# Seven 128x128 products in place of four 128x256 in a projection, reciprocals spread by DMA, one score tile lowered by VectorE

## The chip, the cores and the metric

The kernel runs on one core of a Trainium2 chip. The metric is the device time of one execution in microseconds (us); lower is better. The kernel before the change takes 997.76 us, the median of three runs.

In what follows PE is TensorE, DVE is VectorE, ACT is ScalarE, POOL is GpSimd and SP is SyncE, which here only issues DMAs. PSUM is the memory that PE writes; DVE and ACT can read it, POOL cannot. SBUF is the working memory of all of them.

## The reference

A cross-attention block in fp32, for 16 batches of 1024 query rows and 64 context rows, width 512, 16 heads of 32:

```
xq  = (1 + scale_q) * layernorm(x)       + shift_q     # scale, shift from silu(cond) @ Wss
xkv = (1 + scale_kv) * layernorm(ctx)    + shift_kv
q = xq @ Wq + bq ;  k, v = split(xkv @ Wkv + bkv)
p = softmax(q k^T / sqrt(32))                          # per head, over 64 keys
out = x + ((p v) as rows of 512) @ Wp + bp
```

## The kernel before, in words

**Blocks.** The query rows are cut into 32 blocks of 512 rows, two to a batch. A block passes through these steps: normalise (`hidden`, ACT), transpose (`turn` on DVE and `move`, 16 DMAs), scale (`scale_features`, ACT), query projection (`query_product`, `quarter_products`, PE), scores (`score_products`, PE), maxima (`maximum` and `maxima`, DVE), subtraction of the maxima (`subtract`, POOL), exponentials (`weights` and `again`, ACT), the sum over the keys (`total` on POOL, `row_total` on DVE), the product with the values (`mix`, PE), the division by the sum (`divided`, DVE) and the output projection (`product`, PE, with `added` on DVE).

**Fewer products.** Each 512x512 projection is cut into halves and made by a scheme with seven half-size products instead of eight. Products are numbered 1 to 7. Their operands include sums and differences of halves, which POOL makes (`row_sum` for the rows `ot`, `feature_sums` for the features), and their results are added up in PSUM in a fixed order. In the output projection products 1, 6, 5 and 3 go into PSUM bank 2 one after the other, products 2, 7 and 4 into bank 3. After each product `added(i, n)` (DVE, L1116) adds the bank's present content to the output rows `r`, and the next product into that bank waits until `added` has read it. Query products 1 and 7 are already made a second time by this scheme, of seven 128x128 products each: `quarter_products`, with operands from `feature_quarters` (POOL), a copy by ACT (`quarter_copies`) and three adds by DVE in PSUM (`quarter_adds`), before the last three of the seven run. The weight sums for query product 7 are made once, ahead of the loop, by POOL (`weight_quarter_sums(7)`, L565 to L573).

**Loop.** Lines L1587 to L1704 run for i = 3 to 29. An iteration works on several blocks at once: the scores of block i, the output projection of block b = i-2 (products 6, 5, 4, 3) and a = i-1 (products 1, 2, 7), the query projection of block n = i+1, and the preparation of blocks i+2 to i+4. Ahead of the loop the same steps stand written out for blocks 0 to 3, behind it for blocks 30 and 31.

**Order.** The order of the calls in the source is the order of each engine's queue; nothing reorders it. An engine takes its instructions strictly in that order, so an instruction that waits holds all behind it on the same engine. The same holds for the DMAs that SP issues.

**Around the scores.** A block's score tile has two key halves z = 0 and 1, and each lies in two PSUM tiles (e = 0 and 1). There are only two such PSUM tiles in turn; the next `score_products` or `mix` needs them back. They come back when DVE has taken the maxima (L755, 128x1024 at a time) and ACT has copied the scores to SBUF (`copied`, L764). `maxima` then spreads the maxima over 128x2048 (`mb`, L784, a DVE transpose), POOL subtracts `mb` from both halves (L797, 128x2048 each), ACT takes the exponentials, POOL adds the halves (`total`, L858), DVE reduces the sum (`row_total`, L863) and takes its reciprocal (L878).

**Reciprocals.** `inverse_rows` writes the 128x64 reciprocals to DRAM (32 KB) and reads them back in another order (four DMAs of 8 KB into `vr`); `spread_rows`, in the next iteration, spreads them over 128x2048 by a DVE transpose (L891) into `vb`. `divided` (L915, two instructions of 128x1024) multiplies the PSUM result of `mix` by `vb` and leaves `ot` in SBUF.

## Time and profile before

| what | value |
|---|---|
| median of three runs | 997.76 us (997.4 to 999.06) |
| the profiled execution: time / span in the trace | 999.01 us / 996.9 us |
| busy share of the span: PE, DVE, ACT, POOL | 99%, 90%, 78%, 90% |
| first scores of the loop (block 3) on PE | 151.2 us from the span's start |
| one iteration, from block to block | 28.52 us |
| first scores behind the loop (block 30) on PE | 921.4 us |

In rows of the trace the columns are: start in us, duration in us, engine, line, operation, output<-inputs, partitions times elements, count; in brackets the idle time of the engine just before, and what ended it. Rows that stand directly behind one another can be merged ("x2"). In the chain of waits a row is start, duration and what the end of the program hung on at that time. One PE product of the source shows as two records, so "x8" is four products.

### The profile page before, as it was taken

The numbers are of one execution on the slowest core, as the hardware profiler recorded it, in microseconds if no ns is written. First come the engines' busy times: TensorE is split into PE (matmuls) and PEld (weight loads), VectorE is DVE, ScalarE is ACT, GpSimd is POOL, SyncE is SP. The second block draws the span as 40 slices with busy tenths as digits, with TensorE's granted clock in tenths as the row PEclk, the third lists the DMA queues.
The fourth block names the chain that finished last, engine by engine and source line by source line (L and its number), as shares of the span: only waits on it lengthen the run. The fifth ranks groups of instructions, "written<-read, shape, count | busy, mean of one in ns | idle before, by whom it ended". The sixth has DMA issues, their size and how long they took to land.

```text
span 996.9 us, 20564 instructions
## 1 busy us (share of the span) xinstructions
PE 984.2 (99%) x7465; PEld 760.7 (76%) x7465; DVE 895.6 (90%) x1318; ACT 779.3 (78%) x1165; POOL 895.4 (90%) x690
## 2 busy tenths in 40 slices
PE   7999999999999999999999999999999999999998
PEld 6878777787777877877778778777787787777756
DVE  7696899999999999999999999999999999987786
ACT  3878878888888888888888888888888888876620
POOL 2677899999999999999999999999999999999681
PEclk9999999999999999999999999999999999999999
DMA  9765655555655555566655555665555555544422
GB/s 308 264 165 151 156 164 156 140 165 180 190 181 176 159 165 152 151 182 186 183 176 152 173 145 155 185 188 178 176 150 175 151 154 182 148 132 130 145 85 97
DMA packets 115188, 165.77 MB, mean 166 GB/s; under 512 B 34920, under 2 KB 46464, under 8 KB 113168
## 3 DMA queue, kind: packets, MB, share of 16 engines
q1 hardware_dynamic: 114704, 163.93, 55.2%
q8 instruction: 59, 0.97, 0.4%
q0 software_dynamic: 384, 0.54, 0.2%
q14 instruction: 41, 0.34, 0.1%
HBM read 79.47 MB, written 34.60 MB: 114 GB/s over the span
## 4 chain that ended last, share of the span: by engine, by line
PE 88%; DMA 4%; DVE 3%; SPq 2%; POOL 1%; issue 1%; ACT 0%; DVEq 0%; POOLq 0%
PE pp L1086 36%; PE pq L534 27%; PE pq L605 10%; PE ps L738 6%; PE po L936 5%; PE pk_A L534 1%; PE pk_B L534 1%; DMA w_k_sb<-in_L_xcond_Wkv_dram 1%; DMA r<-in_x_dram 1%; PE pv_B L534 1%; DMA ltd<-lt 1%; DMA V_B<-stage_B 1%; DMA vr<-ltd 0%; POOL sum L858 0%; DVE l L826 0%
## 5 line engine op out<-in xcount | busy, mean ns | idle before, releaser
L797 POOL TENSOR_TENSOR s<-s,mb 128x2048 f32<-128x2048 f32 x64 | 290.6, 4564 | 20.3 <-DVE mb L784 13.4
L1086 PE MATMUL pp<-w_p_sb,ot 128*128 128x256 f32 x740 | 174.8, 379 | 1.1 <-DVE ot L915 1.1
L764 ACT COPY s<-ps 128x1024 f32<-128x1024 f32 x128 | 129.3, 1013 | 46.1 <-PE ps L738 34.0
L755 DVE TRANSPOSE_TENSOR_REDUCE m<-ps 128x32 f32<-128x1024 f32 x128 | 152.4, 1228 | 10.4 <-PE ps L738 9.3
L1086 PEld LDWEIGHTS pp<-w_p_sb,ot 128*128 128x128 f32 x740 | 138.2, 190 | 20.5 <-issue 2.8
L645 ACT ACTIVATE qt<-pq,bias_t 128x256 f32<-128x256 f32 x256 | 107.8, 475 | 48.8 <-PE pq L605 27.7
L858 POOL TENSOR_TENSOR sum<-s,p 128x2048 f32<-128x2048 f32 x30 | 136.5, 4549 | 1.6 <-ACT p L808 1.6
L1116 DVE TENSOR_TENSOR r<-pp,r 128x512 f32<-128x512 f32 x183 | 120.3, 669 | 13.8 <-ACT xt L442 6.8
L534 PE MATMUL pq<-xt,w_q_sums 128*128 128x256 f32 x512 | 123.8, 385 | 0.0
L534 PEld LDWEIGHTS pq<-xt,w_q_sums 128*128 128x128 f32 x512 | 95.0, 190 | 34.6 <-issue 22.6
L1086 PE MATMUL pp<-WT,ot 128*128 128x256 f32 x492 | 118.4, 383 | 0.0
L1086 PE MATMUL pp<-WT,s 128*128 128x256 f32 x488 | 116.1, 380 | 1.3 <-DVE r L1107 0.8
L817 ACT ACTIVATE s<-s 32x2048 f32<-32x2048 f32 x60 | 114.6, 1910 | 1.8 <-DMA p<-s 0.4
L1086 PEld LDWEIGHTS pp<-WT,ot 128*128 128x128 f32 x492 | 90.9, 190 | 19.1 <-issue 4.2
L1086 PEld LDWEIGHTS pp<-WT,s 128*128 128x128 f32 x488 | 88.2, 190 | 13.1 <-POOL s L1056 1.3
L327 ACT ACTIVATE x<-x,rstdq 128x512 f32<-128x512 f32 x128 | 94.8, 807 | 1.0 <-POOL rstdq L304 1.0
L442 ACT ACTIVATE xt<-xt,ss_q 128x512 f32<-128x512 f32 x124 | 94.0, 809 | 1.0 <-DMA xt<-ht 0.7
L915 DVE TENSOR_TENSOR ot<-po,vb 128x1024 f32<-128x1024 f32 x62 | 73.0, 1219 | 17.6 <-PE po L936 17.4
L286 DVE BATCH_NORM_STATS2 bs<-x 128x6 f32<-128x512 f32 x128 | 85.3, 666 | 0.0
L493 POOL TENSOR_TENSOR xt_sums<-xt 128x512 f32<-128x512 f32 x64 | 81.2, 1269 | 2.0 <-DMA x<-in_x_dram 1.3
L357 DVE STREAM_TRANSPOSE ht<-x 128x512 f32<-128x512 f32 x124 | 77.7, 679 | 4.7 <-DMA xt<-ht 2.2
L891 DVE STREAM_TRANSPOSE vb<-vr 128x2048 f32<-128x2048 f32 (+1 forms) x33 | 73.7, 2236 | 4.4 <-DMA vr<-ltd 4.4
(224 smaller groups left out, 1963.8 us busy)
## 6 DMA issues: line engine op xcount, KB each, us to landing
x<-in_x_dram SPq DMA_DIRECT2D x32, 1024.0 KB, 5.3
r<-in_x_dram SPq DMA_DIRECT2D x32, 1024.0 KB, 5.9
xt<-ht SPq DMA_DIRECT2D x488, 64.0 KB, 2.0
out_dram<-r SPq DMA_DIRECT2D x60, 512.0 KB, 4.7
p<-s SPq DMA_DIRECT2D x60, 256.0 KB, 3.8
wss_kv<-in_L_xcond_Wss_kv_dram SPq DMA_DIRECT2D x4, 512.0 KB, 7.2
wss_q<-in_L_xcond_Wss_q_dram SPq DMA_DIRECT2D x4, 512.0 KB, 11.0
vr<-ltd SPq DMA_DIRECT2D x128, 8.0 KB, 1.7
```

Source lines behind the costliest of these rows:

```text
L327: nc.scalar.activation(dst, src, AF.Identity, bias=rstd[:, 1, j : j + 1], scale=rstd[:, 0, j : j + 1])
L442: nc.scalar.activation(xt[:, :, c, :], xt[:, :, c, :], AF.Identity, scale=ss["q"][:, c, b : b + 1], bias=ss["q"][:, NC + c, b : b + 1],)
L534: nc.tensor.matmul(out_, lhsT=lhsT, rhs=rhs, start=new and m == 0 and c == 0, stop=c == HC - 1, skip_group_check=True,)
L605: nc.tensor.matmul(qa["q", k][:, q * P : (q + 1) * P], lhsT=lhsT, rhs=rhs, start=first and q == 0, stop=True, skip_group_check=True,)
L645: nc.scalar.activation(dst, src, AF.Identity, bias=bq_t[:, o : o + 1])
L755: nc.vector.tensor_reduce(m_tiles[i][:, z, 2 * e : 2 * e + 2, :], s_banks[i, z][e].rearrange("p r (j a) -> p r j a", a=32), AX.X, ALU.max, ...
L764: nc.scalar.copy(s_tiles[i, z][:, 2 * e : 2 * e + 2, :], s_banks[i, z][e])
L797: eng.tensor_tensor(s_tiles[i, z], s_tiles[i, z], mb_tiles[i], ALU.subtract)
L817: nc.scalar.activation(s_tiles[i, 0][at + 32 : at + 64], raw_tiles[i][at : at + 32], AF.Exp, scale=SCALE)
L858: nc.gpsimd.tensor_tensor(t, s_tiles[i, 0], s_tiles[i, 1], ALU.add)
L1086: nc.tensor.matmul(to, lhsT=rows[:, c, t * P : (t + 1) * P], rhs=cols[:, c, :], start=n == 2 and (i, 2) not in seeded and t == 0 and c == ...
L1116: nc.vector.tensor_add(r, a, r)
```

## The change

1. **Output product 1 of blocks 2 to 28** is made of seven 128x128 products (`row_products`, four first and three later) in place of four 128x256. Its operands are made per block by POOL (`row_quarters`, three instructions); ACT copies two quarters of the bank (`row_copies`), DVE adds three times in PSUM (`row_adds`). The bias that fills bank 2 is reordered for that (`bias_quarters`). Four weight sums for it are made once, ahead of the loop, by DVE (`projection_quarter_sums`), and `weight_quarter_sums(7)` moves from POOL to DVE and stands earlier.
2. **Reciprocals of blocks 2 to 29**: DVE transposes the 128x64 reciprocals, one DMA writes them to DRAM (32 KB), and `spread_rows` reads them back by four DMAs of 256 KB, each value to the 32 partitions and all places where it is needed. The DVE transpose of 128x2048 goes.
3. **One score tile**: for z = 1 and e = 0, DVE subtracts `mb` straight from PSUM (`lowered`, 128x1024); the ACT copy of that tile goes, and POOL's subtraction for z = 1 is halved (`subtract_half`, 128x1024).
4. `row_sum(i, 2)` writes into a part of `ot` that is no longer needed instead of a tile of its own. The order of the calls in the loop is written anew; `added(b, 7)` now opens an iteration. Some calls ahead of the loop change places. Behind the loop all of the first two row groups of `w_p` and the bias are loaded again, and the DVE transpose for block 29 is gone.

```
+    def lowered(i, e):
+        es = slice(2 * e, 2 * e + 2)
+        nc.vector.tensor_tensor(
+            s_tiles[i, 1][:, es, :], s_banks[i, 1][e], mb_tiles[i][:, es, :], ALU.subtract
+        )
...
     def inverse_rows(i):
         lt = lt_tiles.pop(i)
         nc.vector.reciprocal(lt, lt)
...
+        if by_dram(i):
+            t = v.rearrange("p c j -> p (c j)")
+            nc.vector.transpose(t, lt.rearrange("p r j -> p (r j)"))
+            d = rows_dram[i] = dram.tile([2, NC, 2, TB], F32, tag="lb", name=f"lb_{i}")
+            nc.sync.dma_start(
+                d.rearrange("k c e (j a) -> (c e j) k a", a=32),
+                t.rearrange("p (k a) -> p k a", k=2),
+            )
+            return
...
     def spread_rows(i, cs=range(NC)):
+        if by_dram(i):
+            d = rows_dram.pop(i)
+            vb = vb_tiles[i] = qpool.tile([P, NC, TB], F32, tag="vb", name=f"vb_{i}", bufs=1)
+            for r in range(HPC):
+                row = d[r // 2, :, r % 2, :].unsqueeze(0)
+                nc.sync.dma_start(vb[32 * r : 32 * r + 32], row.to_broadcast([32, NC, TB]))
+            return
...
+    def projection_quarter_sums():
+        tt, w = nc.vector.tensor_tensor, p_quarters
+        tt(w[:, 0], weight_block(0, 1), weight_block(0, 0), ALU.subtract)
+        tt(w[:, 2], weight_block(1, 1), weight_block(0, 1), ALU.add)
+        tt(w[:, 1], weight_block(0, 0), w[:, 2], ALU.subtract)
+        tt(weight_block(0, 1), weight_block(1, 0), w[:, 1], ALU.add)
...
+    def row_quarters(i):
+        tt, x, r = nc.gpsimd.tensor_tensor, lambda t, c: row_block(i, t, c), r_quarters
...
+        tt(r[:, 0:2], x(1, 0).unsqueeze(1).to_broadcast([P, 2, P]), others, ALU.subtract)
+        tt(r[:, 2], r[:, 1], x(0, 0), ALU.subtract)
+        tt(ident, x(0, 1), r[:, 2], ALU.add)
...
+    def row_products(i, first):
+        x, r, w = lambda t, c: row_block(i, t, c), r_quarters, p_quarters
+        if first:
+            todo = (
+                (0, x(0, 0), weight_block(0, 0)),
+                (1, r[:, 1], w[:, 0]),
+                (2, r[:, 0], w[:, 2]),
+                (3, r[:, 2], w[:, 1]),
+            )
+        else:
+            todo = (
+                (0, x(0, 1), weight_block(1, 0)),
+                (1, ident, weight_block(1, 1)),
+                (2, x(1, 1), weight_block(0, 1)),
+            )
...
+    def row_adds(i):
+        a, r, tt = acc[2], r_quarters, nc.vector.tensor_tensor
+        both_ = a[:, P : 3 * P].rearrange("p (k n) -> p k n", k=2)
+        tt(r[:, 2], a[:, 3 * P :], r[:, 0], ALU.add)
+        tt(both_, both_, r[:, 2:3].to_broadcast([P, 2, P]), ALU.add)
+        tt(a[:, 3 * P :], a[:, 2 * P : 3 * P], r[:, 1], ALU.add)
...
     query_out(3, 2)
+    weight_quarter_sums(7, nc.vector)
     query_out(3, 6)
...
     added(1, 1)
+    projection_quarter_sums()
     scale_features(4, (0,))
```

**DVE ahead of the loop, first place.** The queue between `added(0, 6)` and the spreading of block 1's reciprocals; `BN_STATS` and `BN_AGGR` are `q_stats` of block 6, the `TENSOR_TENSOR` into `r` is `added`. Before:

```order
L1116 TENSOR_TENSOR r_1130<-pp_2_1225,r_1130 128x2x256
L286 BN_STATS bs<-x_1248 128x6
L287 BN_AGGR mvq_1384<-bs 128x2
L286 BN_STATS bs<-x_1248 128x6
L287 BN_AGGR mvq_1384<-bs 128x2
L286 BN_STATS bs<-x_1248 128x6
L287 BN_AGGR mvq_1384<-bs 128x2
L286 BN_STATS bs<-x_1248 128x6
L287 BN_AGGR mvq_1384<-bs 128x2
L1116 TENSOR_TENSOR r_1130<-pp_2_1225,r_1130 128x2x256
```

And now, from the first of the four `BN_STATS` on:

```order
L284 BN_STATS bs<-x_1250 128x6
L285 BN_AGGR mvq_1385<-bs 128x2
L568 TENSOR_TENSOR w_p_sb<-w_q_sums 128x128
L569 TENSOR_TENSOR w_p_sb<-w_p_sb,w_q_sums 128x128
L570 TENSOR_TENSOR w_p_sb<-w_q_sums 128x128
L571 TENSOR_TENSOR w_p_sb<-w_q_sums,w_p_sb 128x128
L284 BN_STATS bs<-x_1250 128x6
L285 BN_AGGR mvq_1385<-bs 128x2
L284 BN_STATS bs<-x_1250 128x6
L285 BN_AGGR mvq_1385<-bs 128x2
L284 BN_STATS bs<-x_1250 128x6
L285 BN_AGGR mvq_1385<-bs 128x2
```

The four sums of `weight_quarter_sums(7)`, whose inputs both lie in SBUF, stand ahead of three of the four statistics and so ahead of `added(0, 5)`, the row that follows them.

**DVE ahead of the loop, second place.** From `added(1, 1)` to the first maximum of block 3; `qt` is `query_added(3, 4)`, `lt` the row total of block 2 and its reciprocal. Before:

```order
L1116 TENSOR_TENSOR r_1154<-pp_2_1470,r_1154 128x2x256
L652 TENSOR_TENSOR qt_1388<-pq_7_1451,qt_1388 128x2x4x32 x2
L1116 TENSOR_TENSOR r_1154<-pp_2_1484,r_1154 128x2x256
L863 TENSOR_REDUCE lt_1506<-sum_1489 128x64
L878 RECIPROCAL lt_1506<-lt_1506 128x64
L755 TENSOR_REDUCE m_3_1580<-ps_0_0_1562 128x32
```

Now:

```order
L1224 TENSOR_TENSOR r_1156<-pp_2_1475,r_1156 128x2x256
L1142 TENSOR_TENSOR p_quarters<-w_p_sb 128x128
L1143 TENSOR_TENSOR p_quarters<-w_p_sb 128x128
L1144 TENSOR_TENSOR p_quarters<-w_p_sb,p_quarters 128x128
L1145 TENSOR_TENSOR w_p_sb<-w_p_sb,p_quarters 128x128
L650 TENSOR_TENSOR qt_1389<-pq_7_1456,qt_1389 128x2x4x32 x2
L1224 TENSOR_TENSOR r_1156<-pp_2_1493,r_1156 128x2x256
L874 TENSOR_REDUCE lt_1515<-sum_1498 128x64
L894 RECIPROCAL lt_1515<-lt_1515 128x64
L898 STREAM_TRANSPOSE vr_1518<-lt_1515 128x64
L1224 TENSOR_TENSOR r_1156<-pp_3_1513,r_1156 128x2x256
L753 TENSOR_REDUCE m_3_1588<-ps_0_1_1571 128x32
```

Four sums with both inputs in SBUF come between `added(1, 1)` and `query_added(3, 4)`. The small transpose and `added(b, 7)` come between the reciprocal and the first maximum; these two stand there in every iteration of the loop as well.

**POOL in the loop.** The queue of iteration 15 from the first subtraction on. Before (two subtractions, two row sums, the sum of the halves):

```order
L797 TENSOR_TENSOR s_0_4821<-s_0_4821,mb_4878 128x2048
L797 TENSOR_TENSOR s_1_4854<-s_1_4854,mb_4878 128x2048
L1051 TENSOR_TENSOR s_14_4962<-ot_4956 128x512
L1053 TENSOR_TENSOR ot_4956<-ot_4956 128x2x256
L858 TENSOR_TENSOR sum_4992<-s_0_4821,p_4979 128x2048
```

Now:

```order
L795 TENSOR_TENSOR s_0_4937<-s_0_4937,mb_4994 128x2048
L808 TENSOR_TENSOR s_1_4971<-s_1_4971,mb_4994 128x1024
L1161 TENSOR_TENSOR r_quarters<-ot_5057 128x256
L1162 TENSOR_TENSOR r_quarters<-r_quarters,ot_5057 128x128
L1163 TENSOR_TENSOR ident<-ot_5057,r_quarters 128x128
L1087 TENSOR_TENSOR s_14_5072<-ot_5057 128x512
L1089 TENSOR_TENSOR ot_5057<-ot_5057 128x2x256
L869 TENSOR_TENSOR sum_5126<-s_0_4937,p_5099 128x2048
```

The second subtraction is half as wide, and three instructions for the row quarters stand ahead of the row sums and the sum of the halves.

251 lines of the change are left out of this document (145 added, 106 removed).

## The prediction

> **What bounds the kernel now.** I read the page's first part, then the chain of waits, then the timeline of one iteration (492 to 521 us) engine by engine, then the timeline ahead of the loop.
>
> ```profile
> PE 984.2 (99%) x7465; PEld 760.7 (76%) x7465; DVE 895.6 (90%) x1318; ACT 779.3 (78%) x1165; POOL 895.4 (90%) x690
> 491.87 1.79 PE pp L1086 x8
> 520.39 1.79 PE pp L1086 x8
> 492.00:520.52 28.52, 28.52 (x222) 22.15 (x221) 27.00 (x40) 24.00 (x36) 27.53 (x22) 1.00 0.57 170
> ```
>
> PE is busy 99% of the span, and in the chain its last product of one iteration starts 28.52 us after that of the iteration before. The last row is one such stretch: PE 28.52, DVE 27.00, ACT 24.00, POOL 27.53 us busy, at a granted clock of 1.00. So PE sets the pace, but POOL and DVE have only 1 to 1.5 us to spare. Busy shares don't say whether these two also form a chain from one iteration to the next. They do (DVE, POOL, DVE in the rows):
>
> ```profile
> 494.89 2.39 DVE L755 TRANSPOSE_TENSOR_REDUCE m<-ps 128x32 f32<-128x1024 f32 x2 [0.27 <-PE ps L738]
> 504.01 9.08 POOL L797 TENSOR_TENSOR s<-s,mb 128x2048 f32<-128x2048 f32 x2 [0.27 <-ACT qt L645]
> 520.23 2.31 DVE L863 TRANSPOSE_TENSOR_REDUCE lt<-sum 128x64 f32<-128x2048 f32 x1
> ```
>
> From the first maximum (494.89) DVE works without a gap to `mb`, and POOL's subtraction starts 9.12 us later. POOL then subtracts twice, makes two row sums and the sum, and DVE's `row_total` starts 16.22 us after that (520.23). The next maximum comes at 494.89 + 28.52 = 523.41, 3.18 later, of which DVE idles 0.27 until PE has the scores. So this chain is 28.25 us long: 0.27 shorter than PE's.
>
> **The change part by part: PE.**
>
> ```profile
> 504.67 0.89 PE pq L605 x8
> 509.02 0.67 PE pq L605 x6
> 513.49 1.73 PE pp L1086 x8
> ```
>
> Product 1 (513.49) takes 1.73 us on PE. The same scheme in query product 7 takes 0.89 for the first four products and 0.67 for the last three, 1.56. That is 0.17 less per block, and 28.35 us per iteration. Over 27 blocks, with PE still setting the pace: -4.6 us. Nothing else leaves PE.
>
> **The chain of DVE and POOL in the loop.**
>
> ```profile
> L797 POOL TENSOR_TENSOR s<-s,mb 128x2048 f32<-128x2048 f32 x64 | 290.6, 4564 | 20.3 <-DVE mb L784 13.4
> L493 POOL TENSOR_TENSOR xt_sums<-xt 128x512 f32<-128x512 f32 x64 | 81.2, 1269 | 2.0 <-DMA x<-in_x_dram 1.3
> 492.88 0.73 POOL L581 TENSOR_TENSOR t_quarters<-xt 128x256 f32<-128x256 f32 x1
> 494.64 1.27 POOL L493 TENSOR_TENSOR xt_sums<-xt 128x512 f32<-128x512 f32 x1
> L784 DVE STREAM_TRANSPOSE mb<-m 128x2048 f32<-128x2048 f32 x32 | 74.0, 2312 | 1.1
> L357 DVE STREAM_TRANSPOSE ht<-x 128x512 f32<-128x512 f32 x124 | 77.7, 679 | 4.7 <-DMA xt<-ht 2.2
> L915 DVE TENSOR_TENSOR ot<-po,vb 128x1024 f32<-128x1024 f32 x62 | 73.0, 1219 | 17.6 <-PE po L936 17.4
> ```
>
> - POOL's halved subtraction: between 512 elements (1269 ns) and 2048 (4564) an element costs 2.145 ns, so 1024 cost 2.37 us, and 2.20 go.
> - `row_quarters` has the shapes of `feature_quarters`: 492.88 to 494.64, so 1.76 us are added, ahead of the sum.
> - DVE's small transpose stands behind the reciprocal: on the line through 2048 (2312) and 512 elements (679), 0.20 us for 64.
> - `added(b, 7)` now stands between this and the maximum: an L1116 of 0.69 (rows below); instructions that don't depend on one another overlap by nearly 0.1, so 0.6.
>
> The chain becomes 28.25 - 2.20 + 1.76 + 0.20 + 0.60 = 28.61 us, 0.26 longer than PE's new 28.35 and 0.09 longer than the period now. I take 28.6: 27 times 0.08 is +2.2 us. `lowered` (like L915, 1.22 us from PSUM) replaces the big transpose outside this chain; `row_adds` have the widths of `quarter_adds` and stand there too. PE's 0.26 of slack hides the copy by ACT between the two parts of `row_products`.
>
> **Ahead of the loop** lies the larger term. Eight sums of 128x128 go to DVE with both inputs in SBUF. In the loop of before DVE has no such instruction: each sum reads PSUM. Elsewhere there are a few:
>
> ```profile
> 981.94 0.67 DVE L1051 TENSOR_TENSOR s<-ot 128x512 f32<-128x512 f32 x1
> 982.72 1.79 DVE L1056 TENSOR_TENSOR s<-ot,s 128x512 f32<-128x512 f32 x1
> 982.70 1.27 POOL L1053 TENSOR_TENSOR ot<-ot 128x512 f32<-128x512 f32 x1 [12.74 <-DVE s L1051]
> 19.67 1.64 DVE L493 TENSOR_TENSOR xk_A<-xk_A 128x512 f32<-128x512 f32 x1
> 19.24 1.52 POOL L467 TENSOR_TENSOR w_k_sums<-w_k_sums,w_k_sb 128x512 f32<-128x512 f32 x1 [1.16 <-DMA w_k_sb<-in_L_xcond_Wkv_dram]
> 20.72 1.71 POOL L467 TENSOR_TENSOR w_k_sums<-w_k_sb 128x512 f32<-128x512 f32 x1
> ```
>
> With POOL idle the first takes 0.67 us. The second, the same shape, begins 0.02 after a POOL instruction and takes 1.79: it ends 0.54 after POOL's end (983.97). The third ends (21.31) 0.55 after POOL's end (20.76). POOL's next, queued at 20.72, lasts 1.71 where 1.27 is usual. So they don't share: DVE's sum stands until POOL's instruction ends, then goes first. No row has this against a long POOL instruction; I take it that DVE waits as long as that lasts. (The Trainium skill, SBUF — State Buffer, "Who interferes with whom", says it outright: a DVE instruction with two SBUF inputs contends with a POOL instruction that reads SBUF, and the loser is blocked for the whole instruction. The rows above agree; the sum goes by the rows.)
>
> ```profile
> 131.18 4.54 POOL L797 TENSOR_TENSOR s<-s,mb 128x2048 f32<-128x2048 f32 x1
> 135.68 1.30 POOL L493 TENSOR_TENSOR xt_sums<-xt,xt_sums 128x512 f32<-128x512 f32 x1
> 136.92 4.56 POOL L797 TENSOR_TENSOR s<-s,mb 128x2048 f32<-128x2048 f32 x1
> 132.57 0.68 DVE L286 BATCH_NORM_STATS2 bs<-x 128x6 f32<-128x512 f32 x1
> 135.77 0.66 DVE L1116 TENSOR_TENSOR r<-pp,r 128x512 f32<-128x512 f32 x1
> 139.82 2.35 DVE L915 TENSOR_TENSOR ot<-po,vb 128x1024 f32<-128x1024 f32 x2
> 137.18 1.99 PE L1086 MATMUL pp<-WT,ot 128*128 128x256 f32 x8
> 144.19 3.65 PE L1086 MATMUL pp<-w_p_sb,ot 128*128 128x256 f32 x16
> ```
>
> *First four.* DVE reaches them at 133.4 (132.57 plus one statistic, 0.8), with POOL in a subtraction until 135.72. Taking 0.2 us for a 128x128 sum: the first ends at 135.9; POOL's next (1.30) at 137.2, the second sum at 137.4; POOL's second subtraction (4.56) at 142.0, the third sum at 142.2; then POOL has to wait for `divided(1)`, and the fourth ends at 142.4. (If POOL went first each time, DVE would wait until POOL runs dry, at 141.5: nearly the same end.) DVE has lost 9.0 us. `added(0, 5)` moves from 135.77 to 144.8 and ends at 145.5; product (0, 3) on PE (137.18) adds to the same bank behind it and starts at 145.6, 8.4 us late. Nothing covers that. `divided(1)` moves to 148.8 and is then in time, so product (1, 1) stands at 144.19 + 8.4 = 152.6.
>
> ```profile
> 144.03 4.56 POOL L858 TENSOR_TENSOR sum<-s,p 128x2048 f32<-128x2048 f32 x1
> 148.54 0.74 POOL L581 TENSOR_TENSOR t_quarters<-xt 128x256 f32<-128x256 f32 x1
> 146.22 0.69 DVE L1116 TENSOR_TENSOR r<-pp,r 128x512 f32<-128x512 f32 x1 [1.00 <-ACT xt L442]
> 147.88 0.69 DVE L1116 TENSOR_TENSOR r<-pp,r 128x512 f32<-128x512 f32 x1 [0.30 <-PE pp L1086]
> 152.53 2.38 DVE L755 TRANSPOSE_TENSOR_REDUCE m<-ps 128x32 f32<-128x1024 f32 x2 [1.00 <-PE ps L738]
> 148.60 0.59 ACT L1031 COPY pp<-b_diff 128x512 f32<-128x512 f32 x1 [1.69 <-DVE r L1116]
> 149.41 1.90 PE L1086 MATMUL pp<-WT,ot 128*128 128x256 f32 x8
> ```
>
> *Second four.* `added(1, 1)` (146.22) follows product (1, 1), which now ends at 154.3, so DVE is done with it at 155.0. POOL's sum follows `divided(1)`: from 144.03 to 152.7, ending at 157.3. The four sums then end at 157.5, 158.4, 159.0 and 159.7, each behind one POOL instruction (4.56, then 0.74 and two of 0.46, as `feature_quarters` has them). With `query_added` (0.7) `added(1, 2)` starts at 160.4 and ends at 161.1, where it ended at 148.57: +12.5. ACT's copy of the bias (148.60) and product (1, 7) (149.41) wait for it and move as far, and `row_total(2)` starts at 161.1. From there 2.91 us (3.18 less the idle 0.27) + 0.20 + 0.60 to the first maximum of the loop: 164.8, or 165.0 with the scores behind product (1, 7). It was 152.53: +12.5 us. The loop has no slack to make that up, on PE or in the chain.
>
> **Queues and the rest.**
>
> ```profile
> x<-in_x_dram SPq DMA_DIRECT2D x32, 1024.0 KB, 5.3
> 492.95 8.89 SPq L382 DMA_DIRECT2D xt<-ht  x12
> ```
>
> SP issues as many DMAs as before (1 + 4 a block) but reads 1 MB a block. The small write now waits for DVE ahead of all 16 moves of the block, which delays the first 12; nothing needs them before the next iteration's scaling. `vb` is issued some 7 us into the iteration, behind 8 moves (8.89 us for 12 in the row), and at the row's 5.3 us lands around 12 to 13; `divided` needs it 14 to 15 us in. Behind the loop PE sets the pace at first and DVE has gaps, so the transpose saved there brings nothing. These count zero.
>
> **The sum**, against the profiled execution's own time (span 996.9, time 999.01): 999.0 + 12.5 + 2.2 = 1013.7. That execution stood 1.25 above the median, so 1012.5 by the median. I say 1012.
>
> **Rivals.**
> - *No blocking at that length; PE sets the pace* (faster). DVE's eight sums run at their own 0.3 us, mostly covered by DVE's idle 1.00 + 0.30 + 1.00 at 146 to 153, and the new chain is under 28.35: 997.8 - 4.6 = 993. It decides from 0.26 us off my 28.61. For it: rows show the block only against POOL instructions of 1.3 us. Against: three cases of three. Chance 0.12.
> - *No blocking, the chain as I add it up*: 997.8 + 2.2 = 1000, between 998 and 1002. Chance 0.10.
> - *Blocking, but PE sets the loop's pace*: 997.8 + 12.5 - 4.6 = 1006; and if a sum waits no more than the 1.1 us seen, each group costs 5.2 instead of 9.0 and 4.7, some 8.5 together, 1008 with the chain. Both lie within the forecast's case, as does the next.
> - *PE's clock.* PE would stand still for 8.4 and about 4 us. No row of before has such a gap in the middle of the program; the granted clock was 1.00 in the stretch quoted. Were it halved after the second gap, a product (1.73) and the scores (1.07) ahead of the loop would take 2.8 us more: 1015. (The Trainium skill, TensorE: Matmul & The Clock Gate, Part 1, has the clock halved after about 3.4 us idle; no run here shows it yet.) I give it 1 in 3 within the forecast.
> - *`vb` late.* If the four reads land over 2 us later than I put them, `divided` and POOL's row quarters slip; each 0.1 us then costs 27 times 0.1 = 2.7 us: 1018 and more. Chance 0.08.
>
> **How the numbers follow.** Forecast 0.70, no blocking with PE's pace 0.12, no blocking with the chain 0.10, `vb` late 0.08. A measurement tells about 0.2% (2 us) from no change. Faster by that: 0.12. Within it (995.8 to 999.8): 0.08, most of the second unblocked case. Slower: 0.80. The forecast's own range is 1004 to 1020: the loop from -4.6 to +6 (0.15 us a period on the new prices), 8.5 to 12.5 ahead of it, up to 2.8 for the clock. The stated range adds the unblocked chain: 996 to 1020.
>
> **What would show it.** Right: the first 128x128 sum on DVE ends just behind POOL's subtraction, at about 135.9; PE idle 8 us ahead of product (0, 3); the first maximum of the loop at 165; a period of 28.6 with a short wait of PE at its second scores, for DVE. Wrong: eight DVE sums of 0.3 us each; or a period of 28.35 with DVE idle ahead of the maximum.

## The result, and the profile after

The changed kernel takes 1024.22 us (median of 5 runs, 1023.87 to 1026.19) against 998.36 for the kernel before (now the median of five): ratio 1.0266, 95% interval 1.0254 to 1.0278. The forecast was 1012, with a range of 996 to 1020. The direction and the forecast's largest term, 12.5 us ahead of the loop, came out; the loop cost more than six times what I gave it, 14.3 us for 2.2.

The first part of the page, after:

```profile
PE 995.2 (97%) x7627; PEld 760.4 (74%) x7627; DVE 912.5 (89%) x1434; ACT 771.8 (75%) x1165; POOL 879.7 (86%) x769
```

PE is busy 97% of the span where it was 99%. Of the 27.5 us by which the span is longer, 16.5 show as idle time of PE and 11.0 as busy time (995.2 for 984.2). That busy time is not more work: products take longer at a halved clock, and the modelled end of a product's row covers most of a wait as short as the 0.25 us below. The queue of the DMAs that SP issues moved 192.90 MB in 71.1% of the DMA engines' time, where it was 163.93 MB in 55.2%.

The first scores of the loop and the first behind it in PE's timeline, before (L738):

```profile
151.24 1.14 PE L738 MATMUL ps<-qt,K_A 32*32 32x512 f32 x32
921.40 1.14 PE L738 MATMUL ps<-qt,K_B 32*32 32x512 f32 x32
```

and after (L736):

```profile
163.76 1.55 PE L736 MATMUL ps<-qt,K_A 32*32 32x512 f32 x32
948.24 1.14 PE L736 MATMUL ps<-qt,K_B 32*32 32x512 f32 x32
```

The profiled spans are 996.9 and 1024.4: +27.5, where the medians differ by 25.9; both profiled executions are the longest of their five. Of the 27.5, 12.5 lie ahead of the loop (163.76 - 151.24), 14.3 in its 27 periods (784.48 against 770.16) and 0.7 behind it.

**Ahead of the loop**, the timeline after; the number in front of the engine is the duration, and a wait stands in brackets at the end:

```profile
130.03 4.53 POOL L795 TENSOR_TENSOR s<-s,mb 128x2048 f32<-128x2048 f32 x1
135.82 4.55 POOL L795 TENSOR_TENSOR s<-s,mb 128x2048 f32<-128x2048 f32 x1
132.23 2.48 DVE L568 TENSOR_TENSOR w_p_sb<-w_q_sums 128x128 f32<-128x128 f32 x1
135.94 4.59 DVE L570 TENSOR_TENSOR w_p_sb<-w_q_sums 128x128 f32<-128x128 f32 x1
140.45 0.28 DVE L571 TENSOR_TENSOR w_p_sb<-w_q_sums,w_p_sb 128x128 f32<-128x128 f32 x1
143.76 3.78 PE L1121 MATMUL pp<-WT,ot 128*128 128x256 f32 x8 [7.67 <-DVE r L1224]
160.68 3.15 PE L1121 MATMUL pp<-WT,ot 128*128 128x256 f32 x8 [2.63 <-ACT pp L1067]
165.68 2.38 DVE L753 TRANSPOSE_TENSOR_REDUCE m<-ps 128x32 f32<-128x1024 f32 x2 [1.05 <-PE ps L736]
```

The first and third sum end 0.15 and 0.16 us behind POOL's two subtractions (134.56 and 140.37). A sum that takes 0.28 us by itself takes 4.59. PE then waits 7.67 us for product (0, 3), which runs at half pace (3.78 us, 1.89 elsewhere). The granted clock is 0.50 from 140.83 to 147.66 and again from 161.31 to 164.72, and 1.00 between; product (1, 7) at 160.68 and the first scores fall into the second stretch.

**A plain iteration** of the loop, timeline after:

```profile
261.86 1.59 PEld L1121 LDWEIGHTS pp_2q<-WT,ot 128*128 128x128 f32 x8 [0.22 <-DVE r L1224]
261.87 1.98 PE L1121 MATMUL pp_2q<-WT,ot 128*128 128x256 f32 x8
269.05 0.39 PE L1182 MATMUL pp_2q<-w_p_sb,ot 128*128 128x128 f32 x2
269.27 0.83 PE L1182 MATMUL pp_2q<-p_quarters,r_quarters 128*128 128x128 f32 x6
269.94 1.89 PE L532 MATMUL pq<-xt,w_q_sums 128*128 128x256 f32 x8
270.20 0.38 ACT L1193 COPY r_quarters<-pp_2q 128x256 f32<-128x256 f32 x1
270.68 0.29 DVE L1199 TENSOR_TENSOR r_quarters<-pp_2q,r_quarters 128x128 f32<-128x128 f32 x1 [0.19 <-ACT r_quarters L1193]
271.47 0.30 DVE L1201 TENSOR_TENSOR pp_2q<-pp_2q,r_quarters 128x128 f32<-128x128 f32 x1
271.92 0.46 PE L1182 MATMUL pp_2q<-w_p_sb,ot 128*128 128x128 f32 x2
272.66 1.89 PE L532 MATMUL pq<-xt_sums,w_q_sb 128*128 128x256 f32 x8
```

Product 1 takes PE 0.89 us for the first four (269.05 to 269.94) and 0.74 for the last three (271.92 to 272.66). Between them stand the copy by ACT and three additions by DVE, done at 271.77; query product 5, which should cover them, is over at 271.67, one product time of 1.73 after its start. PE loses 0.25 us there and 0.10 ahead of product 3 (261.87), which waits for `added(b, 5)`. The row of query product 5 ends only at 271.83 and so hides most of the first wait. PE loses nothing else, and a plain period is 28.78 us against 28.52.

**An irregular iteration**, the chain of waits after:

```profile
479.28 8.85 DMA p<-s
488.16 0.03 ACT s L828
490.08 1.52 ACT x L325 x2
491.60 0.49 ACT pq L544
492.13 1.99 PE pq L532 x8
```

`p<-s` is the swap of the score halves (`swapped`, 2 x 256 KB). It lands 8.85 us after the sum that releases it; ACT's exponential `again` waits for it, behind that the query seed, and PE for the seed. In the table of waits:

```profile
ACT s L828 <- DMA p<-s: 8.6, 7, 2.4
```

Seven waits, 8.6 us together. Summed over all 27 periods, what exceeds 28.78 is 7.4 us. The loop's 14.3 us are therefore 27 x 0.26 = 7.0 and these 7.4, less 0.1 that the kernel before has too.

Of the 7.4 us, 5.9 lie in the five iterations in which PE then waits for the seed; their swaps land 8.4 to 10.0 us after the issue. In one of them (from 686.44) the inverse rows are late as well, behind the same swap, and DVE's division waits 1.3 us for them. The first period has 0.6 us, mostly its scores at the halved clock; the rest is small.

### The profile page after: what moved, and what is told of

The parts are those of the page before. It is cut to its first block, busy times and chain, and to the rows that moved or that the text cites. A ratio compares the mean times of both kernels' runs of the same rounds, so it can differ in the third digit from the quotient of the medians.

```text
span 1024.4 us, 21138 instructions
## 1 busy us (share of the span) xinstructions
PE 995.2 (97%) x7627; PEld 760.4 (74%) x7627; DVE 912.5 (89%) x1434; ACT 771.8 (75%) x1165; POOL 879.7 (86%) x769
## 3 DMA queue, kind: packets, MB, share of 16 engines
q1 hardware_dynamic: 118432, 192.90, 71.1%
## 4 chain that ended last, share of the span: by engine, by line
PE 64%; POOL 11%; DVE 9%; DMA 8%; ACT 3%; issue 3%; SPq 1%; POOLq 0%; DVEq 0%; ACTq 0%
PE pq L532 21%; PE pp L1121 11%; PE pp_2q L1121 9%; PE pq L603 6%; DMA p<-s 5%; PE ps L736 5%; PE po L968 4%; POOL s L795 4%; PE pp_2q L1182 3%; POOL sum L869 3%; DVE m L753 2%; DVE mb L782 2%; POOL s L808 1%; PE pk_A L532 1%; PE pk_B L532 1%
## 5 line engine op out<-in xcount | busy, mean ns | idle before, releaser
L795 POOL TENSOR_TENSOR s<-s,mb 128x2048 f32<-128x2048 f32 x37 | 168.4, 4556 | 44.1 <-DVE mb L782 38.1
L762 ACT COPY s<-ps 128x1024 f32<-128x1024 f32 x101 | 101.9, 1013 | 55.6 <-PE ps L736 44.6
L1121 PE MATMUL pp<-w_p_sb,ot 128*128 128x256 f32 x524 | 123.7, 379 | 0.4 <-DVE ot L947 0.4
L1121 PEld LDWEIGHTS pp<-w_p_sb,ot 128*128 128x128 f32 x524 | 99.3, 190 | 15.7 <-issue 1.9
L1121 PE MATMUL pp_2q<-WT,ot 128*128 128x256 f32 x432 | 104.2, 384 | 0.0
L1121 PEld LDWEIGHTS pp_2q<-WT,ot 128*128 128x128 f32 x432 | 78.3, 190 | 15.0 <-DVE r L1224 5.5
L1121 PE MATMUL pp<-WT,ot 128*128 128x256 f32 x304 | 77.5, 399 | 11.5 <-DVE r L1224 7.7
L355 DVE STREAM_TRANSPOSE ht<-x 128x512 f32<-128x512 f32 x124 | 82.8, 688 | 5.7 <-ACT x L325 2.2
L819 ACT ACTIVATE s<-s 128x2048 f32<-128x2048 f32 x34 | 65.0, 1912 | 17.6 <-POOL s L795 17.5
L1121 PEld LDWEIGHTS pp<-WT,ot 128*128 128x128 f32 x304 | 56.6, 195 | 27.8 <-DVE r L1224 8.9
L532 PEld LDWEIGHTS pq<-xt_sums,w_q_sums 128*128 128x128 f32 x296 | 54.2, 191 | 29.8 <-issue 22.6
```

Of the source, the lines that this page charges most:

```text
L355: nc.vector.transpose(ht_tiles[i][:, :, :, t, :].rearrange("p k c b -> p c k b"), x_tiles[i][:, t, :].rearrange("p (c k b) -> p c k b", c= ...
L532: nc.tensor.matmul(out_, lhsT=lhsT, rhs=rhs, start=new and m == 0 and c == 0, stop=c == HC - 1, skip_group_check=True,)
L762: nc.scalar.copy(s_tiles[i, z][:, 2 * e : 2 * e + 2, :], s_banks[i, z][e])
L795: eng.tensor_tensor(s_tiles[i, z], s_tiles[i, z], mb_tiles[i], ALU.subtract)
L1121: nc.tensor.matmul(to, lhsT=rows[:, c, t * P : (t + 1) * P], rhs=cols[:, c, :], start=n == 2 and (i, 2) not in seeded and t == 0 and c == ...
```

## The experiments

First the numbers of all runs, from PE's timeline as above; "excess" is the 27 periods less 27 times the plain one. In the three kernels marked with a star hardly a period is plain, and the 28.78 of the kernel after is used.

| kernel | first scores | 27 periods | plain period | excess | median us, ratio to before (95%) |
|---|---|---|---|---|---|
| before | 151.24 | 770.16 | 28.52 | 0.1 | 998.36 |
| after | 163.76 | 784.48 | 28.78 | 7.4 | 1024.22, 1.0266 (1.0254 to 1.0278) |
| sums_on_pool | 150.26 | 784.10 | 28.78 | 7.0 | 1011.74, 1.0145 (1.0129 to 1.0161) |
| before_sums_on_vector | 160.17 | 770.06 | 28.52 | 0.0 | 1007.85, 1.0099 (1.0084 to 1.0114) |
| sums_on_pool_four_products | 149.70 | 791.09 | 29.12 | 4.9 | 1015.95, 1.0178 (1.0161 to 1.0195) |
| four_products_second_place | 149.86 | 789.59 | 29.13 | 3.1 | 1015.07, 1.0158 (1.0142 to 1.0173) |
| copy_ahead | 150.72 | 791.39 | 29.11 | 5.4 | 1017.58, 1.0189 (1.0174 to 1.0205) |
| no_quarter_additions | 149.72 | 775.00 | 28.52 | 5.0 | 1002.42, 1.0049 (1.0034 to 1.0064) |
| product3_behind_quarter7 | 149.51 | 817.23 | 29.95 | 8.6 | 1044.44, 1.0473 (1.0458 to 1.0489) |
| swap_before_x | 164.24 | 801.27 | 28.78* | 24.2 | 1042.40, 1.0439 (1.0418 to 1.0461) |
| second_exponential_late | 162.90 | 782.43 | 28.78 | 5.4 | 1021.98, 1.0227 (1.0209 to 1.0245) |
| small_output | 163.04 | 781.30 | 28.78 | 4.2 | 1020.69, 1.0238 (1.0222 to 1.0253) |
| x_behind_first_move | 164.16 | 810.10 | 28.78* | 33.0 | 1049.49, 1.0517 (1.0492 to 1.0542) |
| x_earlier | 164.20 | 778.17 | 28.78 | 1.1 | 1019.29, 1.0211 (1.0196 to 1.0226) |
| quarters_from_block_4 | 149.98 | 779.79 | 28.78 | 2.7 | 1007.26, 1.0095 (1.0078 to 1.0112) |
| quarters_4_x_behind_move | 149.60 | 807.04 | 28.78* | 30.0 | 1035.37, 1.0370 (1.0322 to 1.0418) |
| quarters_4_x_earlier | 151.15 | 779.45 | 28.78 | 2.4 | 1006.54, 1.0084 (1.0067 to 1.0101) |
| all_repairs | 150.16 | 962.28 | 33.6 to 36.6 | | 1190.22, 1.1921 (1.1903 to 1.1940) |

**Is it the sums on VectorE?** One run moves them away in the kernel after, one puts four of them into the kernel before.

```
 # sums_on_pool
-    weight_quarter_sums(7, nc.vector)
...
-    projection_quarter_sums()            # on nc.vector
...
     feature_sums(4, nc.gpsimd, (2,))
+    weight_quarter_sums(7)               # on nc.gpsimd
+    projection_quarter_sums()            # on nc.gpsimd
```

> The kernel after, with the eight 128x128 sums (the four weight quarters of product 7 and the four projection quarters) issued on POOL, behind the second feature sum of block 4, and no longer on VectorE. Theory (VectorE's sums over two SBUF inputs stand still while POOL runs a subtraction of 4.55 us, and everything in front of the loop waits for them): the first score maximum of the loop goes from 165.7 us back to 152 to 154, the whole from 1024.2 to about 1012 (1010 to 1014), the period of the loop stays 28.8 and its irregular iterations stay. Rival (the head is late because its other steps were moved, the sums only lie where the wait shows): the first maximum stays above 160 and the whole above 1020.

```
 # before_sums_on_vector: the kernel before
     query_out(3, 2)
+    weight_quarter_sums(7, nc.vector)
     query_out(3, 6)
...
-    weight_quarter_sums(7)
```

> The kernel before, with one part of the change alone: the four weight quarters of product 7 summed on VectorE, two steps ahead of product 5 of block 0, as in the kernel after. Theory (these four stand still behind POOL's two subtractions and cost what they cost in the kernel after, about 9 us, most of it passed on to the loop): 1006 to 1008 against 998.4, the first score maximum of the loop at 160 to 162 instead of 152.5. Rival (four sums of 0.3 us beside idle time): 998 to 1000.

Both came out as the theory had it: 1011.74, and 1007.85. In the kernel before, the four sums show the same times as in the kernel after, and the first maximum moves from 152.53 to 161.46:

```profile
132.19 2.48 DVE L570 TENSOR_TENSOR w_p_sb<-w_q_sums 128x128 f32<-128x128 f32 x1
135.90 4.59 DVE L572 TENSOR_TENSOR w_p_sb<-w_q_sums 128x128 f32<-128x128 f32 x1
161.46 2.47 DVE L755 TRANSPOSE_TENSOR_REDUCE m<-ps 128x32 f32<-128x1024 f32 x2 [1.16 <-PE ps L738]
```

So the first four cost 8.9 us by themselves, with the clock that they bring: it is 0.50 from 138.37 to 148.61 in this run too. sums_on_pool had one cost that was not foreseen: POOL spends 3.7 us on the eight sums (157.39 to 161.06) and so starts its subtraction late, and the first period is 33.1 us:

```profile
171.68 1.65 PE L1182 MATMUL pp_2q<-p_quarters,r_quarters 128*128 128x128 f32 x6 [2.87 <-POOL r_quarters L1161]
```

**What sets the period?** Two kernels go back to four products at different places, one moves ACT's copy, one leaves the additions out, one moves product 3. All build on sums_on_pool.

```
 # sums_on_pool_four_products (row_quarters, row_copies, row_adds go)
-        row_products(a, True)
+        product(a, 1)
         query_out(n, 7)
         query_product(n, 5)
-        row_products(a, False)
```

> As sums_on_pool, with product 1 again made as four 128x256 products at the place where the first of the seven stood, without the row quarters on POOL, the copy on ScalarE and the three additions on VectorE, and without the projection's and the bias's quarters. The rest of the change stays. Theory (in the steady iterations TensorE sets the period of 28.78 us; the seven products take 0.89 and 0.74 us and a wait of 0.25 us for VectorE's additions, 1.88 in all, against 1.73 for four): the period goes to 28.6, and the whole is 4 to 5 us below sums_on_pool, about 1007.5. Rival (the chain from POOL's subtraction to VectorE's maximum sets the period): 2.8 us less on it makes the period 28.5 or less, and with TensorE's 28.5 as the next bound the whole is 7 us or more below sums_on_pool. Second rival (the seven products gain what was meant, 0.17 us a block): the whole is 4 us above sums_on_pool.

```
 # four_products_second_place
-        row_products(a, True)
         query_out(n, 7)
         query_product(n, 5)
-        row_products(a, False)
+        product(a, 1)
```

> As sums_on_pool_four_products (1015.95 us; period 29.12, since query product 5 ends 0.9 us later there and VectorE's additions behind it end in front of product 7), with the four products of product 1 at the place of the second half of the seven, behind query product 5. Theory (TensorE's own row is the bound of sums_on_pool, 0.89 + 0.74 us and a wait of 0.25 us against 1.73): the period is 28.63 and the whole 4 us below sums_on_pool, about 1007.7; then the seven products lose 0.15 us a block where they were to gain 0.17. Rival (the seven products gain what was meant): the whole stays 3 us or more above sums_on_pool, over 1014.5.

My theory missed in both: the plain period is 29.12 and 29.13, and the whole 4.2 and 3.3 us above sums_on_pool, as the rivals had it. But the rows show waits that the order makes. At the first place PE waits ahead of product 7, since DVE's additions to the query products come late; at the second, query product 5 waits for a bank that the first four products had covered. From the timelines of the first and of the second kernel:

```profile
353.20 1.97 PE L1121 MATMUL pp<-WT,ot 128*128 128x256 f32 x8 [0.34 <-ACT pp L1067]
```

```profile
314.12 1.99 PE L532 MATMUL pq<-xt,w_q_sums 128*128 128x256 f32 x8 [0.26 <-ACT qt L643]
```

In the second kernel PE's query product 5 starts at 314.12, 0.43 us after the end of the product ahead of it (313.47 + 0.22). With this gap and 0.1 of restart taken off, 29.13 becomes 28.6. That is an estimate of PE's work with four products in this order; no run shows it. The order around the seven products was made for them, so taking only them out is no clean test of their price.

```
 # copy_ahead
+        row_copies(a)
         query_out(n, 7)
         query_product(n, 5)
-        row_copies(a)
         row_adds(a)
```

> As sums_on_pool (1011.7 us), with one step moved in each block: ScalarE copies the first two quarters of product 1 (0.37 us) ahead of its two passes over query output 7 (1.57 us with output 6) and not behind them. Theory (TensorE, which is never idle otherwise in the steady iterations, stands 0.25 us ahead of the second half of product 1 for VectorE's three additions, and those start 0.2 us late for this copy): the additions start at 0.18 us earlier, the period goes from 28.79 to 28.6, the whole to about 1007 (1006 to 1009). Rival (VectorE is the bound, TensorE's 0.25 us would come back as another wait): under 1.5 us gained. Second rival (the copy waits for all four products of the half): no gain, or up to 2 us lost, since query output 7 comes later.

5.8 us lost. The second rival was near: the copy waits for PE on ACT (0.84 us each time), but the price is paid elsewhere. ACT's second exponential comes later, and POOL's sum waits for it. From the table of waits:

```profile
ACT r_quarters L1193 <- PE pp_2q L1182: 22.7, 27, 1.6
POOL sum L869 <- ACT p L819: 16.8, 28, 1.3
```

The chain of waits of this kernel no longer runs through PE but from DVE's maxima to POOL, its sum and DVE's `row_total`, 29.11 us round, of which POOL waits 0.60 for ACT. Without that wait it would be 28.5 us long, which the next run bears out.

```
 # no_quarter_additions
         row_copies(a)
-        row_adds(a)
```

> As sums_on_pool (1011.7 us), with VectorE's three additions between the two halves of product 1 left out (so product 1 is not complete); everything else, the copy too, stays. TensorE's second half then waits for nothing that is made between the halves. Theory (in sums_on_pool TensorE's row is the bound, and 0.25 us of wait and 0.07 us of weight loads behind it are the price of these additions): the period goes from 28.79 to 28.5, where the chain from POOL's subtraction through the sum to VectorE's maximum is the next bound (28.52 by the rows of copy_ahead), the whole to 1004 to 1005.5. Rival (the time of the three additions on VectorE counts, not the wait: 1.0 us a block on a VectorE that is 27.4 us busy): over 1.0 us per block gained, under 990. Second rival (another wait takes its place at once): under 2 us gained.

The plain period is 28.52, as the theory had it, and 1002.42 is 9.3 us below sums_on_pool, 1.6 us below the forecast: 26 x 0.26 = 6.8, the rest in the first period (31.8 for 33.1) and in fewer irregular ones. PE's wait for the additions was the bound, and 0.26 us behind it lies the chain: the chain of waits of this run holds no PE, only POOL's subtraction to DVE's maxima and back (POOL's subtractions start at 334.97 and 363.50). DVE reaches `row_total` early in every block and waits for POOL:

```profile
DVE lt L874 <- POOL sum L869: 14.3, 28, 1.2
```

```
 # product3_behind_quarter7
-        product(b, 3)
-        added(b, 3)
         query_out(n, 2)
-        copied(i, 1, 1)
         quarter_products(n, 7, True)
+        product(b, 3)
+        added(b, 3)
+        copied(i, 1, 1)
```

> As sums_on_pool, with TensorE's product 3 of the block before moved behind the first half of query quarter product 7, and ScalarE's copy of the second score tile behind query output 2 and ahead of nothing else. Theory (product 3 waits 0.1 us for the addition of product 5, which VectorE reaches only behind the spreading of the maxima; the quarter product of 0.98 us covers it): the period goes from 28.79 to 28.69, 2 to 3 us gained, about 1009. Rival (product 3 then ends 1 us late for VectorE's addition and the bias copy behind it, and with them for the additions of query quarter 7 and for the division): the period over 29, 6 us or more lost.

The rival holds: period 29.95, +33 us. Product 3's bank must be read by DVE and filled with the bias by ACT before ACT comes to the query outputs, and PE stands for those (POOL's row quarters wait for the later division):

```profile
ACT pp_2q L1056 <- DVE r L1224: 56.2, 27, 2.1
POOL r_quarters L1161 <- DVE ot L947: 29.4, 26, 2.7
PE pq L603 <- ACT qt L643: 27.0, 27, 1.3
```

**All at once**, before these were known one by one:

```
 # all_repairs: copy_ahead, product3_behind_quarter7, second_exponential_late, quarters_from_block_4, and
         score_products(i, 0)
-        added(b, 7)
...
         subtract(i, zs=(0,))
+        added(b, 7)
         added(b, 5)
```

> The kernel after with every cost repaired that the runs showed: weight quarters of product 7 on POOL ahead of the loop; product 1 in seven products from block 4 on only, with the projection's and bias's quarters made on POOL at the end of the second loop iteration; the copy ahead of query output 7; the second exponential late; the addition of product 7 behind the maxima; product 3 behind the first half of query quarter product 7. Theory (all that stood against the change are these waits, and TensorE's row is then 28.36 us a block): the period 28.4 to 28.5, the whole 995 to 1000, equal to the kernel before or 3 us below it. Rival (VectorE, busy 27.4 of 28.8 us, or POOL's chain is the next bound at 28.6 or more): 1002 to 1006.

1190 us, which neither the theory nor the rival had: I had overlooked what `added(b, 7)` releases. Products 7 and 4 share bank 3, so PE's product 4 waits in every block until DVE has spread the maxima (91.2 us together), and runs at half pace in 24 of 27 blocks:

```profile
444.21 3.65 PE L1121 MATMUL pp<-w_p_sb,ot 128*128 128x256 f32 x8 [3.37 <-DVE r L1224]
```

So the 0.60 us that my prediction added to the chain for this instruction are not to be had by this move. As this kernel also holds the two moves that lost on their own, it is no test of the rest.

**Why does the swap land late?**

```
 # swap_before_x
-            load_x(i + 5)
...
         swapped(i)
+            load_x(i + 5)
```

> The kernel after, with one step moved in the loop: the two DMAs that swap the halves of the scores (256 KB each) are issued ahead of the load of the next x (1 MB) instead of behind it. In 7 iterations ScalarE's second exponential waits for this swap, which lands 7.5 to 10 us after the sum that releases it; the iterations with an end later than 28.8 us cost 8.7 us together. Theory (the swap stands in the DMA engines behind the 1 MB that was issued 0.7 us ahead of it): it lands within 5 us, no iteration waits for it, the whole goes from 1024.2 to about 1015.5 (1014 to 1018). Rival (the engines are behind by the whole of the traffic that the 1 MB of the inverse rows adds, whatever the order of these two): under 3 us gained, over 1021, and the waits for the swap stay or go over to the x that now comes later.

18 us lost. The swap lands in 3.6 us (median), and but for one wait of 0.3 us no instruction waits for it any more; they wait for other transfers. The chain of waits, with the loads in one period:

```profile
312.10 9.18 DMA x<-in_x_dram
321.29 0.51 SPq L380
324.07 5.70 DMA vb<-lb
```

A move of `xt` on SP (L380) does not use this x, yet SP waits there until x has landed, 25 times, 54.4 us. By its place it is the eighth DMA behind x. Behind it in SP's queue stand the reads of the inverse rows (`vb`), and DVE's division (329.90) waits for those. This was the rival "`vb` late" of my prediction.

```
 # second_exponential_late
-        again(a, 0)
...
         query_seed(n)
+        again(a, 0)
         product(b, 4)
```

> The kernel after, with ScalarE's first exponential of the swapped half put behind the hidden units and the query seed, 1.9 to 2.0 us later in ScalarE's row; no DMA is moved. Theory (the swap lands late in some iterations and ScalarE then holds up the query seed, for which TensorE waits; 7 waits of 8.6 us together): what lands up to 2 us late costs nothing now, 7 to 8 us are gained, 1016 to 1018 against 1024.2. Rival (the swap lands the later the faster the loop runs, since the DMA engines are the bound): under 3 us gained, the waits for the swap become longer.

```
 # small_output, blocks 2 to 28
-                rows_of(out, i)[:, 2 * m : 2 * m + 2, :], ...
+                rows_of(out, i)[:, 2 * m : 2 * m + 2, :64], ...
```

> The kernel after, in which the two output DMAs of each of the blocks 2 to 28 write 64 of the 512 columns (64 KB each and not 512 KB), so that the output of these blocks is not complete; their number, order and waits are the same, and the traffic of a block is 0.9 MB less, nearly what the inverse rows' 1 MB added. Theory (the irregular iterations of the kernel after, 7.4 us over the period of 28.78 together, come from the DMA engines, which move 5.5 MB a block instead of 4.5 and deliver the swap and the inverse rows late): every iteration takes 28.75 to 28.9, no instruction waits for the swap, the whole is 1015.5 to 1018 against 1024.2. Rival (the SP queue's order and its waits for earlier DMAs make them late, not the bytes): under 2.5 us gained.

2.2 and 3.5 us gained by the medians (3.9 and 2.8 by the ratios to the kernel before). The first is less than the theory had and near the rival's 3 us, the second lies between theory and rival. The excess was 5.4 and 4.2 for 7.4; in sums_on_pool, whose loop is that of the kernel after, it was 2.7 without the first period. So it varies among kernels with the same loop by as much as these gains, and the times decide nothing.

The rows say more. In small_output, with 0.9 MB less in a block, ACT still waits for the swap (3.8 us, five times), so fewer bytes of output don't remove the wait. In second_exponential_late ACT never waits for it, but the swap is as late as before, and in three of the irregular iterations the chain of waits goes from it through SP's queue: a move of `xt` waits for the swap, the inverse rows are read late, and DVE's division, POOL's row quarters and PE (0.26 us here) wait:

```profile
623.74 9.08 DMA p<-s
632.84 0.58 SPq L380
636.59 5.90 DMA vb<-lb
642.61 1.24 DVE ot L947
```

```
 # x_behind_first_move
-            load_x(i + 5)
...
             move(i + 3, ks=(0,))
+            load_x(i + 5)
```

> The kernel after, with the load of the next x (1 MB) issued behind the swap, the write of the inverse rows and the first four moves of xt, 3.9 to 5 us later than in the kernel after. There x is issued 0.7 us ahead of the swap on engines that had been idle for about 3 us, because its buffer comes free only at VectorE's fourth transposition of the block; in swap_before_x the third of the next moves waited for that x and held up the inverse rows. Theory (it is the meeting of these two transfers that makes the swap late, and a move eight DMAs behind a transfer waits for it): the swap lands within 5 us, only the last of the four reads of the inverse rows waits for x; the iterations with more than 28.85 us fall from 7.4 us of excess to under 2, the whole to 1017 to 1019. Rival (the 5.5 MB of a block are late in one place or another): the inverse rows or x come late instead, 1023 or more.

25 us lost, as the rival had it, and again for the reason above: here the eighth DMA behind x is the last read of the inverse rows, and SP waits there for x. From SP's waits:

```profile
SPq L917 <- DMA x<-in_x_dram: 47.6, 24, 5.7
```

SP's rows hold the clue. Issues of x and of the swap, before:

```profile
459.43 0.38 SPq L119 DMA_DIRECT2D x<-in_x_dram  x1
463.20 1.15 SPq L813 DMA_DIRECT2D p<-s  x2
```

after:

```profile
478.59 0.38 SPq L119 DMA_DIRECT2D x<-in_x_dram  x1
479.28 1.15 SPq L824 DMA_DIRECT2D p<-s  x2
```

Before, 1 MB of x had 3.77 us ahead of the swap; after, 0.69, and it is much the same in nearly every block (3.3 to 4.5 before, 0.5 to 0.8 after). x waits on SP for its buffer, which DVE's fourth transposition (`ht`, L355) frees:

```profile
SPq L119 <- DVE ht L355: 164.7, 28, 6.7
```

The new order of the fuller DVE has this transposition later in the block. So the last test leaves SP's order alone and lets DVE transpose earlier:

```
 # x_earlier
         query_product(n, 4)
-            q_stats(i + 4, (3,))
...
-        query_added(n, 4)
             turn(i + 3, (3,))
             load_x(i + 5)
+        query_added(n, 4)
+            q_stats(i + 4, (3,))
         added(a, 2)
```

> The kernel after, with three steps of VectorE in another order: the last three transpositions of x (they free its buffer) ahead of the second query addition and of the fourth statistics of the next block, which come behind them. The SP queue's order is unchanged, but the load of the next x is released 1.3 to 1.6 us earlier. In the kernel before x is issued 3.77 us ahead of the swap, in the kernel after 0.70 us, in no_quarter_additions (no wait for the swap there) 1.2 us. Theory (the swap is late because x's 1 MB is issued right ahead of it): x is issued 2 us ahead, no instruction waits for the swap, the excess of the iterations over 28.8 us falls from 7.4 to under 3 us, the whole to 1017 to 1020. Rival (the irregular iterations have another cause): no gain, 1022 or more, or a loss because the query addition comes late.

The theory holds: x goes out 2.15 us ahead of the swap, the table of waits has none for the swap, the excess falls from 7.4 to 1.1 us, the median from 1024.22 to 1019.29.

```profile
303.65 0.38 SPq L119 DMA_DIRECT2D x<-in_x_dram  x1
305.80 1.15 SPq L824 DMA_DIRECT2D p<-s  x2
```

The excess alone would be thin evidence, since it varies so much among equal loops. The time from the swap's issue to its landing is better, over the loop and for those of its DMAs whose landing the trace gives (6 to 50 of some 50): the longer x's lead, the sooner the swap lands, but for two kernels with nearly the same lead.

| kernel | x ahead of the swap, us | swap's landing, us: shortest, median, longest |
|---|---|---|
| second_exponential_late (the SP order of after) | 0.7 | 6.9, 7.4, 8.8 |
| copy_ahead | 1.3 | 6.2, 6.9, 9.3 |
| no_quarter_additions | 1.2 | 3.1, 6.3, 8.0 |
| x_earlier | 2.15 | 3.1, 4.7, 6.7 |
| before | 3.77 | 3.1, 3.8, 4.5 |
| swap_before_x | behind it | 3.3, 3.6, 5.2 |

So with x 0.7 us ahead the swap is late throughout, and not only where PE waits. In the kernel after ACT comes to it 7.3 us after its issue (277.17 and 284.49), so only what lands later than that costs time.

**What is left of the change?**

```
 # quarters_from_block_4, with second_exponential_late
+    weight_quarter_sums(7)               # nc.gpsimd, as in sums_on_pool
...
-        return 2 <= i < NB - 3
+        return 4 <= i < NB - 3
...
+        if i == 4:                       # end of the iteration
+            projection_quarter_sums()    # nc.gpsimd
+            bias_quarters()
```

> The kernel after, with the weight quarters of product 7 on POOL ahead of the loop, product 1 in seven products from block 4 on only (the projection's and the bias's quarters made on POOL at the end of the second loop iteration), and the second exponential late. Theory (in sums_on_pool the eight sums on POOL, 4.1 us, made the first loop iteration 33.1 us long; here only the first four lie ahead of it, as in the kernel before, and two blocks have TensorE's 1.73 us for product 1): the first iterations cost 3 us less than in sums_on_pool, the loop the same 28.8, the whole about 1008 (1006 to 1010). Rival (POOL pays for the four projection sums in any place, at 2 us): 1010 to 1012. The kernel before, at 998, is not reached by either, for the period stays 0.26 us longer in 25 blocks.

1007.26 and first periods of 29.2, 29.1 and 29.4 where sums_on_pool had 33.1: as the theory had it. With x moved behind the first moves, and the second exponential at its old place, it lost 28 us:

> As quarters_from_block_4 (1007.3 us), with the load of x behind the first four moves as in x_behind_first_move. Theory: that kernel has only 2.7 us of excess in its iterations, so 1 to 2.5 us are gained, 1005 to 1006.5; the rest against the kernel before is 25 periods that are 0.26 us longer, about 6.5 us. Rival as there: 1008 or more.

1035.37, the rival. And with DVE's new order, again with the exponential at its old place (diffs as above):

> As quarters_from_block_4 (1007.3 us), with the same new order on VectorE as in x_earlier. Theory: 2 us of excess are left there, 1 to 2 us are gained, 1005 to 1006.5, and every period is 28.8 or less. Rival: 1007 or more.

1006.54, 0.7 us below quarters_from_block_4: just short of the theory's range, and not every period is plain, as it had it. Five exceed 28.95, together 2.0 us over the plain one; three of these are the first, two of them with four products. This is the best complete version that was found, 0.84% (0.67 to 1.01) slower than the kernel before; none beat that.

## Why the prediction came out as it did

- **Sums ahead of the loop, +12.5: right in the mechanism and in its parts**, and in the total partly by luck. This execution runs 1.15 us earlier there than that of before (`mb` of block 2 at 127.45 for 128.60). With that, the fourth sum was forecast to end at 141.25 and ended at 140.73, the eighth at 158.55 and at 158.65. The total holds two things that the 12.5 left out, of opposite sign: the 1.15 us gained earlier, and the halved clock below. sums_on_pool and before_sums_on_vector show the cause. (The Trainium skill, SBUF — State Buffer, "Who interferes with whom", has the loser blocked for the whole instruction; the trace now agrees with a POOL instruction of 4.55 us.)
- **The clock, given 1 in 3: it came.** Products of 1.89 us took 3.78 and 3.15 behind the two gaps, 3.2 us more, and the first scores 1.55 for 1.14. I had it behind the second gap alone, and it came behind both, also behind one of 2.63 us. Gaps shorter than forecast (7.67 for 8.4, 2.63 for about 4) and the 1.15 us gained earlier made up for most of that, and the first maximum stands at 165.68 where 165.0 was forecast.
- **DVE's and POOL's chain, 28.61: nearly right.** copy_ahead and no_quarter_additions show 28.5. But it is not what sets the period, and the sign that I named, a short wait of PE at its second scores, is not in the rows.
- **PE's row, 28.35: wrong, and here the step failed.** I wrote that "PE's 0.26 of slack hides the copy by ACT between the two parts". The path between the parts is PE, ACT, DVE, PE: and I never laid it beside its cover, one query product of 1.73 us. The copy (0.38) and the additions (1.09) alone would fit; the hand-overs add 0.26 from PE to ACT (269.94 to 270.20), 0.10 to DVE and 0.15 back to PE (271.77 to 271.92): 1.98. PE's own sum is 28.52 - 0.17 + 0.25 (this wait) + 0.07 (three products at 0.74 for 0.67) + 0.10 (product 3 behind `added(b, 5)`) = 28.77. 27 x 0.26 is 7.0 us where I gave 2.2.
- **"These count zero" for SP and its DMAs: wrong, 7.4 us.** I looked at the new DMAs, the inverse rows, and these were late at least once in the loop, behind the swap. What became late was an old one, the swap, because DVE's new order lets x go 3 us later, just ahead of it; the landing times above show it. That is 5.9 of the 7.4 us.
- **The seven products' gain of 0.17 us a block** is there in the work (0.89 + 0.67 for 1.73) and is lost whole in the wait that they bring.

The forecast 12.5 + 2.2 stands against 12.5 + 7.0 + 7.4 + 0.7 (behind the loop). I took the loop's term from 0.08 us a period at the longer of two paths. Both were about 28.5 long (PE's own work 28.35 and 0.10 at product 3), and a third, through PE, ACT and DVE, was 28.78.

What stays open: why the swap lands after 7 us in one iteration and 10 in another although x is 0.7 us ahead of it in all; whether the 0.10 us at product 3 can be had by any order, as the one that was tried lost more; and what parts 2 and 3 of the change bring, for no run takes the inverse rows' way through DRAM or the lowered tile out alone.

## What to carry to other kernels

When one product is cut into two parts with work of other engines in between, add up the whole path from the first part to the second, hand-overs included, and lay it beside what the first engine does meanwhile. When an engine becomes fuller, ask which buffers it now frees later and what their next load will meet on the DMA engines; a late old transfer costs as much as a new one. Small sums with both inputs in SBUF don't belong on DVE while POOL runs long instructions, however idle DVE is.
